# Attention on quarters of TensorE, with the sums' power on GpSimd, and a PSUM pool in the convolution part

## The chip, the cores and the metric

The kernel runs on one core of a Trainium2 chip. A core has engines that work side by side, each with its own queue of instructions that it takes in order: TensorE (called PE in the profile, its weight loads PEld) for matrix products, VectorE (DVE), ScalarE (ACT) and GpSimd (POOL) for work on elements, and SyncE (SP), which here only issues transfers. Data lies in SBUF; TensorE writes its products to PSUM, an accumulation memory of 128 partitions by 4,096 fp32 numbers, in 8 banks of 512. Engines wait for one another by semaphores.

The metric is the time of one execution on the device in microseconds (us). The median of the runs and one profiled execution are given; the profiled execution also has a span, from its first to its last recorded instruction.

## The reference

x has the shape (4, 1024, 256), four sequences of 1,024 tokens of 256 numbers; ctx has (4, 64, 256). Three blocks follow one another, each added to its input and normalised over the 256 numbers (a layer norm):

```python
# 1: Hyena, two long convolutions with gates
r = depthwise_conv3(u @ w_in.T + b_in)        # 768 channels: x0, x1, v
for n in range(2):
    y = irfft(rfft(v, 2048) * rfft(h[n], 2048))[:1024]
    v = y * x_n
out = v @ w_out.T + b_out
# 2: cross attention, 16 heads of 16 numbers, 64 keys
q, k, v = x @ Wq.T + bq, ctx @ Wk.T + bk, ctx @ Wv.T + bv
attn = softmax(einsum('bhqd,bhkd->bhqk', q, k) / 4)
out = einsum('bhqk,bhkd->bhqd', attn, v) @ Wo.T + bo
# 3: gated feed-forward, inner width 1024, with activations
#    rounded to 8 bits and weights to -1, 0, 1 times a scale
out = bitlinear(silu(bitlinear(x, wg)) * bitlinear(x, wu), wd)
```

The filter h of the first block comes from a small network of sines. In the softmax, each sum of 64 exponentials is what the weighted sum of values is divided by.

## The kernel before, in words

**The first part, lines 425 to 850.** The convolution is computed for 8 units (a sequence and half of its channels) by matrix products with tables of sines and cosines. Its stages are: `stage_j` projects and passes the result through memory for the depthwise convolution, `stage_tv` and `stage_tx` transpose, `stage_f` goes to frequencies, `stage_p` multiplies there by the filter on DVE, `stage_i0` and `stage_i1` come back, and `stage_o` applies w_out and the layer norm. The stages of neighbouring units are interleaved by a loop over units. Its instructions are issued straight through the wrapper `Queue.call` (line 61), so their rows in the profile bear L61. An fp32 matrix product takes two passes on TensorE, and the profile has a record for each.

**The second part.** When the loop reaches unit 6 (`u == NU - 2`), `nc.hold()` is called: from here on each instruction is recorded as a `Step` and not issued. The rest of the convolution (the list `rest`) is recorded together with the attention and the feed-forward of 32 tiles of 128 tokens, named by (g, t): g is a group of 512 tokens, t one of its 4 tiles. The functions per tile are:

- `att_q(g)`, line 991, once per group: transposes x1 of four tiles (`turned2`), then computes the queries. `keys(b)`, line 963, builds masked keys of each sequence on DVE, so that heads which share rows of TensorE do not mix.
- `att_s(g, t)`, line 1016: the scores by 4 matmuls, each on 64 of TensorE's 128 rows and 256 moving columns, into 2 banks; the maximum over the 64 keys and the subtraction on DVE; the exponential on ACT. The rows of the profile for these matmuls are `ps_t<-w_in,x0t` and `ps_t<-hf,x0t`, 64x256, the keys being in either buffer.
- `att_v(g, t)`, line 1040: 8 transposes of the exponentials e into PSUM, ACT's copy of them to eT (`vt<-ps_t`), and 8 matmuls with eT as the stationary side and `vblk` as the moving side, 34 columns wide: 2 heads of 16 values and a column of ones each, which gives the sum of weights (`ps_t<-hf,vt` 128x34). DVE takes the reciprocal of the 16 sums of each token (128x16) and multiplies.
- `att_o(g, t)`, line 1077: 2 transposes of the result c (`ps_t<-ident,xt`), ACT's copy to cT (`xc<-ps_t`), the product with Wo, the residual and the layer norm (`norm`, line 1067). The norm's inverse square root is a power of -0.5 on POOL, one number per token: the rows with `mhalf`.
- `ffn_x`, `ffn_h`, `ffn_d`, `ffn_o`: the rounding of the activations, the gate and up products with the silu, the down product, and the last layer norm.

All held instructions are issued by `Engines.go` and bear L82. Their order is not that of the code: `plan` (line 232) is a list scheduler. It takes a cost per instruction from `Step.cost` (line 98), keeps a clock per engine and per PSUM bank (`Clock`), allows an engine to choose among steps that could start within `SLACK`, and prefers low rank; `OFFSET` (line 278) shifts the rank of a stage, and `TABLE_RANK` counts a change of ACT's function table. The order found is written into the engines' queues; on the chip each engine keeps to it and waits at each semaphore.

**PSUM.** One tile `ps_t` holds all 8 banks (line 412). In the first part it is a ring of four pieces of 1,024 columns. In the second, scores have banks 0 and 1; the transposes and the queries banks 2 and 3; the feed-forward's products and the rest of the convolution banks 4 and 5; the small results, named by their first letter (`small`, line 859), bank 6 for a, k, p and bank 7 for the others.

Of the kernel before, what the change touches and what calls it, by code (L numbers as in the profile page):

```python
# [35 lines left out]
NPV = 49  # L36
# [156 lines left out]
class Clock:  # L193


    def __init__(self, steps, before):
        self.steps, self.before = steps, before
        self.free = dict.fromkeys(("PE", "DVE", "ACT", "POOL", "SP"), 0.0)
        self.table = None
        self.bank = [dict.fromkeys(self.free, 0.0) for _ in range(8)]  # L200
        self.end, self.start = [0.0] * len(steps), [0.0] * len(steps)
# [29 lines left out]

def plan(steps, before, rank):
# [11 lines left out]
    for _ in range(n):  # L244
        best = None
        for e, w in wait.items():
            if not w:
# [5 lines left out]
                key=lambda i: (rank[i] + (TABLE_RANK if steps[i].func not in (None, c.table) else 0.0), i),  # L253
# [14 lines left out]
def follow(steps, before, order):  # L268
# [15 lines left out]
def decoder_kernel(  # L284
# [47 lines left out]
    chalf = const.tile([P, 2], FP, name="chalf")  # L332
# [521 lines left out]
    def big(name):  # L854

        o = dict(s=0, t=1024, q=1024, e=1024).get(name[0], 2048)
        return ps_t[:, o : o + 1024]

    def small(name, dtype=FP):
        v = ps_t[:, 3072:3584] if name[0] in "akp" else ps_t[:, 3584:4096]  # L860
        return v if dtype == FP else v.bitcast(dtype)


# [27 lines left out]
    vblk = hfree[0][:, 512 : 512 + B * 8 * 34].rearrange("p (b a e d) -> p b a e d", b=B, a=8, e=2)  # L891

    nc.at = -1
    for dt in range(2):
        ps = small(f"k{dt}")
        for kt in range(2):
            mm(ps[:, 0:256], wk_sb[:, kt, dt * P : dt * P + P], cx[:, kt, :], start=kt == 0, stop=kt == 1)
        act(kT[:, dt, :], ps[:, 0:256], AF.Identity, bias=pv[:, C_BK + dt : C_BK + dt + 1])
    nc.gpsimd.memset(vblk, 0.0)
    for e in range(2):  # L900
        h = slice(64 * e, 64 * e + 64)
        nc.gpsimd.memset(vblk[h, :, :, e, DH : DH + 1], 1.0)
    for b in range(B):
        ps = small(f"v{b}")
        mm(ps[:, 0:256], ones16, brow[:, 2, :], start=True, stop=False)
        for kt in range(2):
            mm(
                ps[:, 0:256],
# [5 lines left out]
        p4 = ps[:, 0:256].rearrange("p (a e d) -> p a e d", e=2, d=DH)  # L914
        for e in range(2):
            h = slice(64 * e, 64 * e + 64)
            nc.scalar.copy(vblk[h, b, :, e, 0:DH], p4[h, :, e, :])
# [9 lines left out]
    r_mx, r_rc, r_am, r_sg, r_hm = stats(NH, 2), stats(NH, 2), stats(3, 4), stats(2, 8), stats(4, 6)  # L927
# [13 lines left out]
    r_c, r_cT = Ring(*parts(xt_t, D)), Ring(*parts(xc_t[1], D))  # L941
# [21 lines left out]
    def keys(b):  # L963

        kb[b] = r_kb().rearrange("p (k h s) -> p k h s", k=2, h=4)
        mk = pv[:, C_MK : C_MK + 4].unsqueeze(2).to_broadcast([P, 4, SKV])
        for dt in range(2):
            tt_(
                kb[b][:, dt],
                kT[:, dt, b * SKV : b * SKV + SKV].unsqueeze(1).to_broadcast([P, 4, SKV]),  # L970
# [4 lines left out]
    def turned2(src, dst, name):  # L975

        ps = big(f"t{name}")
        for kt in range(2):
            for t in range(4):
                nc.tensor.transpose(  # L980
                    ps[:, kt * 512 + t * P : kt * 512 + t * P + P], src[:, t, kt * P : kt * P + P], ident
                )
        nc.scalar.copy(dst.rearrange("p k t -> p (k t)"), ps)
# [7 lines left out]
    def att_q(g):  # L991
# [6 lines left out]
        ps = big(f"q{g}")  # L998
# [17 lines left out]
    def att_s(g, t):  # L1016

        s = gs[g]
        ps = big(f"s{g}_{t}")
# [11 lines left out]
        p3 = ps.rearrange("p (h s) -> p h s", s=SKV)  # L1031
        mx = r_mx()
        nc.vector.tensor_reduce(mx, p3, AX.X, ALU.max)
        e = r_e()[:, 0:1024].rearrange("p (h s) -> p h s", s=SKV)
        tt_(e, p3, mx.unsqueeze(2).to_broadcast([P, NH, SKV]), ALU.subtract)
        ef = e.rearrange("p h s -> p (h s)")
# [3 lines left out]
    def att_v(g, t):  # L1040
        s = gs[g]
        ps = big(f"et{g}_{t}")
        for a in range(8):
            nc.tensor.transpose(ps[:, a * P : a * P + P], s["e", t][:, a * P : a * P + P], ident)
        eT = r_eT().rearrange("p (a q) -> p a q", a=8)
        nc.scalar.copy(eT.rearrange("p a q -> p (a q)"), ps)
        av = small(f"av{g}_{t}")
        for a in range(8):
            mm(
                av[:, a * 34 : a * 34 + 34],  # L1050
                eT[:, a, :],
                vblk[:, g // 2, a].rearrange("p e d -> p (e d)"),
                start=True,
                stop=True,
            )
        a3_ = av[:, 0 : NH * 17].rearrange("p (h d) -> p h d", d=17)
        rc = r_rc()
        nc.vector.reciprocal(rc, a3_[:, :, DH])
        s["c", t] = r_c()
        tt_(  # L1060
            s["c", t].rearrange("p (h d) -> p h d", d=DH),
            a3_[:, :, 0:DH],
            rc.unsqueeze(2).to_broadcast([P, NH, DH]),
            ALU.mult,
        )
# [28 lines left out]
    def ffn_x(g, t):  # L1094
# [16 lines left out]
        ps = small(f"xqT{g}_{t}", F16)  # L1111
# [5 lines left out]
    def ffn_h(g, t):  # L1117
# [3 lines left out]
        for w, k in ((wg_q, 0), (wu_q, 1)):  # L1121
            ps = big(f"p{g}_{t}_{k}")
# [25 lines left out]
    def ffn_d(g, t):  # L1148
        s = gs[g]
        hT = s["hT", t]  # L1150
        po = small(f"po{g}_{t}")
        for c in range(8):
            mm(po[:, 0:D], hT[:, c, :], wd_q[:, c, :], start=c == 0, stop=False)

        mm(po[:, 0:D], neg16, wd_s, start=False, stop=True)
        stt(s["x2", t], po[:, 0:D], s["hs", t], s["x2", t], ALU.mult, ALU.add)
# [23 lines left out]
    space_of["rest"] = ps_t[:, 2048:3072]  # L1180
# [42 lines left out]
def _constants():  # L1223
# [16 lines left out]
    mk = (p[:, None] % 64 // DH == np.arange(4)[None, :]).astype(np.float32)  # L1240
# [67 lines left out]
```

## Time and profile before

| what | value |
| --- | --- |
| median of 3 runs | 764.66 us (764.33 to 764.86) |
| profiled execution, its own time | 765.34 us |
| its span | 763.5 us |
| mean granted TensorE clock | 0.974 |
| busy PE | 710.0 us, 93% |
| busy DVE | 651.4 us, 85% |
| busy ACT | 373.4 us, 49% |
| busy POOL | 150.3 us, 20% |

How to read it. Busy times are shares of the span; TensorE's are modelled, since matrix products are pipelined, so a busy PE need not be at its peak. A row of the groups has the line, the engine and operation, the tiles written and read, the shapes (partitions x elements per partition, type) and the count; behind the first bar the busy time and the mean duration of one in nanoseconds; behind the second the idle time of that engine just before these instructions, and which engine's work ended it. A row of the timeline has the start and the duration in us, and in brackets the idle time before it. Tiles that are used again keep the name of their first use: `small_t` holds the small numbers per token, `xt` the attention's result c, `xc` its transpose, `vt` the transposed exponentials, `tap` the exponentials, `x0t` the queries, `hf` and `w_in` the keys, `hf` also `vblk`, `x1sp` the residual stream.

### The profile page before, as it was taken

To read this page: it belongs to the slowest core of one execution; us is meant where nothing else is said; L and a number is where in the kernel's file an instruction comes from. 1 tells how busy PE (TensorE), PEld (TensorE's weight loads), DVE (VectorE), ACT (ScalarE), POOL (GpSimd) and SP (SyncE) were. 2 spreads that over 40 slices of the span, in tenths; PEclk is the share of its full clock that TensorE was granted. 3 is DMA by queue.
4 is the path that set the end of the run, shared out by engine and by line. 5 is a ranking of instruction groups with operands and counts; after the bars stand their busy time and mean duration, and the time that the engine had idled before them with its cause. 6 is when DMAs were issued, how large, how long until landed. Compare 5 with 4: busy or idle time off the path is not lost. (4 is left out here: it accounts for less than half of the span.)

```text
span 763.5 us, 9645 instructions
## 1 busy us (share of the span) xinstructions
PE 710.0 (93%) x3606; PEld 511.0 (67%) x3606; DVE 651.4 (85%) x1189; ACT 373.4 (49%) x430; POOL 150.3 (20%) x214
## 2 busy tenths in 40 slices
PE   5899599999999999998999999999999999999863
PEld 1346286868687787876788787757676767767631
DVE  3446719999999999599979997989999999999984
ACT  2712516245361525224332213687778777868631
POOL 1210211111121112112000220122222322322322
PEclk9989989999999999999999999999999999999985
DMA  8572553537470644609601000012131322121232
GB/s 282 124 133 110 121 100 65 101 56 142 69 159 16 138 83 82 112 6 177 180 10 55 1 1 1 1 36 49 43 56 36 63 43 63 29 48 41 49 70 48
DMA packets 65140, 57.29 MB, mean 75 GB/s; under 512 B 38500, under 2 KB 49252, under 8 KB 65094
## 3 DMA queue, kind: packets, MB, share of 16 engines
q0 software_dynamic: 13056, 25.17, 19.3%
q1 hardware_dynamic: 47612, 27.84, 14.2%
q10 hardware_dynamic: 4426, 3.68, 1.7%
q8 instruction: 28, 0.46, 0.2%
q14 instruction: 18, 0.15, 0.1%
HBM read 17.34 MB, written 4.19 MB: 28 GB/s over the span
## 5 line engine op out<-in xcount | busy, mean ns | idle before, releaser
L82 PE MATMUL ps_t<-hf 128*128 128x512 bf16 (+1 forms) x512 | 100.3, 334 | 16.6 <-DMA hf<-vf 7.3
L82 PEld LDWEIGHTS <-hf 128*128 128x128 bf16 (+1 forms) x512 | 48.2, 100 | 57.7 <-issue 23.2
L61 PE MATMUL ps_t<-vt,fw 128*128 128x256 f32 x384 | 85.2, 380 | 0.9 <-ACT vt L61 0.6
L61 PEld LDWEIGHTS ps_t<-vt,fw 128*128 128x128 f32 x384 | 72.8, 190 | 13.5 <-issue 2.4
L61 PE MATMUL ps_t<-xt,w_in 128*128 128x512 f32 x168 | 76.4, 607 | 5.1 <-DMA w_in<-in_w_inT 5.1
L61 POOL DMA_DIRECT2D xc<-tap x28 | 33.9, 1245 | 207.1 <-ACT tap L61 133.5
L82 POOL TENSOR_TENSOR small_t<-small_t,mhalf 128x1 f32<-128x1 f32 x64 | 36.4, 574 | 157.6 <-DVE small_t L82 155.7
L82 PEld LDWEIGHTS ps_t<-hf,vt 128*128 128x128 f32 x512 | 61.0, 192 | 8.8 <-DVE small_t L82 3.1
L82 PE MATMUL ps_t<-hf,vt 128*128 128x34 f32 x512 | 61.9, 275 | 1.9 <-DVE xt L82 0.7
L61 PEld LDWEIGHTS ps_t<-xt,w_in 128*128 128x128 f32 x168 | 32.5, 195 | 43.1 <-issue 41.9
L61 ACT ACTIVATE tap<-ps_t,tbias,pv 128x1024 f32<-128x1024 f32 x42 | 48.6, 1210 | 11.4 <-DMA xc<-tap 11.4
L61 DVE TENSOR_TENSOR q<-q 128x1024 f32<-128x1024 f32 x44 | 53.0, 1218 | 0.4
L61 DVE TENSOR_TENSOR q<-vf,hf 128x1024 f32<-128x1024 f32 (+1 forms) x33 | 51.8, 1575 | 0.6
L61 ACT ACTIVATE xc<-ps_t,cbias,pv 128x512 f32<-128x512 f32 x28 | 21.5, 778 | 61.7 <-PE ps_t L61 61.7
L82 DVE SCALAR_TENSOR_TENSOR q<-ps_t,small_t,q 128x1024 f32<-128x1024 f32 x32 | 40.9, 1278 | 7.6 <-PE ps_t L82 4.6
L82 ACT ACTIVATE vf<-q,chalf,small_t 128x1024 f32<-128x1024 f32 x32 | 39.5, 1236 | 15.8 <-POOL small_t L82 8.1
L82 ACT ACTIVATE tap<-tap 128x1024 f32<-128x1024 f32 x32 | 33.8, 1056 | 25.6 <-DVE tap L82 25.4
L61 ACT COPY vo<-ps_t 128x512 f32<-128x512 f32 x24 | 14.0, 585 | 64.1 <-PE ps_t L61 47.4
L61 PE MATMUL ps_t<-q,gi__123 128*128 128x256 f32 x192 | 45.4, 393 | 0.0
L82 ACT ACT_TABLE_LOAD x34 | 43.6, 1283 | 2.2 <-PE ps_t L82 1.6
L82 ACT ACTIVATE q<-ps_t,small_t 128x1024 f32<-128x1024 f32 x32 | 35.6, 1113 | 17.5 <-PE ps_t L82 14.4
L61 DVE TENSOR_TENSOR vf<-ps_t,vo 128x512 f32<-128x512 f32 x48 | 31.1, 683 | 14.7 <-ACT vo L61 14.7
(149 smaller groups left out, 1493.4 us busy)
## 6 DMA issues: line engine op xcount, KB each, us to landing
xc<-tap POOLq DMA_DIRECT2D x32, 512.0 KB, 5.1
x1c<-tap POOLq DMA_DIRECT2D x16, 512.0 KB, 7.1
xt<-in_xT SPq DMA_DIRECT2D x8, 512.0 KB, 6.3
x1sp<-in_x SPq DMA_DIRECT2D x8, 512.0 KB, 4.6
out_y<-v SPq DMA_DIRECT2D x32, 128.0 KB, 1.7
hf<-x1sp SPq DMA_DIRECT2D x3, 512.0 KB, 2.9
fw<-in_dftf SPq DMA_DIRECT2D x1, 1024.0 KB, 14.0
gi__123<-in_dfti SPq DMA_DIRECT2D x1, 1024.0 KB, 10.7
```

The source lines that it names most:

```text
L61: return f(*a, **k)
L82: pin(steps[i].f(*steps[i].a, **steps[i].k))
```

## The change

**PSUM of the first part.** It now comes from a pool `psa` of 4 buffers of 1,024 columns, each asked for at its use. The pool is closed when the loop reaches unit 6, and a second pool with the one tile `ps_t` of 4,096 columns is opened. The held rest of the convolution first takes pieces of it from a ring of four, later from `p_w` alone.

**PSUM of the second part.** Scores `p_s` take the first 256 columns of each of banks 0 to 3 and the transposes `p_t` the last 256. `p_w` is banks 4 and 5. Bank 6 holds `p_num` and `p_den` (`p_xq` lies over `p_den`), bank 7 `p_o` and `p_po`.

**Scores.** 8 matmuls per tile, each on 32 of TensorE's rows with 128 moving columns, the four row quarters into four banks; the masked keys are half as wide. The heads are permuted to suit (`hp` and `mk`).

**Values and sums.** eT is now the moving side, 128 columns, and the stationary side is 32 columns wide: 8 matmuls with `vone` give each head's sum of weights 16 times over, 8 with `vblk` the weighted values, each on one quarter of TensorE's columns. The result lies transposed already. ACT copies the sums, 128x256, to `rd`; POOL raises them to the power -1; DVE multiplies `p_num` by them into cT. The reciprocal on DVE, the 2 transposes of c and ACT's copy of cT are gone.

**Planner.** A change between whole, row-quarter and column-quarter matmuls costs 0.1 or 0.2; a quarter matmul counts a fourth; steps of the same kind are preferred; a wide POOL operation counts 0.52 + 0.002 n, and the constants are others.

```diff
+        self.mode = ""
+        if engine == "PE":
+            self.mode = "rows" if self.ins[0].partition_size() == 32 else "cols" * (self.out.partition_size() == 32)
...
-            if lhs.partition_size() == 64:
-                one *= 0.62
-            return (2 * max(one, 0.112) if rhs.dtype == FP else one), 0.2
+            one = 2 * max(one, 0.112) if rhs.dtype == FP else one
+
+            return (one / 4 if self.mode else one), 0.2
...
-        if self.what == "tensor_copy" or n > 64:
+        if self.what == "tensor_copy":
             return 0.1 + n * 0.00096, 0.06
-        return 0.52, 0.06
+        return 0.52 + n * 0.002 * (n > 64), 0.06
...
+        if e == "PE" and s.mode != self.mode:
+            t += 0.2 if s.mode else 0.1
+            self.mode = s.mode
...
-SLACK = {"PE": 0.00, "DVE": 0.07, "ACT": 0.76, "POOL": 0.0, "SP": 0.0}
-TABLE_RANK = 3.39
+SLACK = {"PE": 0.01, "DVE": 0.07, "ACT": 0.81, "POOL": 0.0, "SP": 0.0}
+TABLE_RANK = 2.89
 OFFSET = dict(
-    att_q=-0.40, att_s=-0.97, att_v=-0.50, att_o=0.40, ffn_x=0.28, ffn_h=-1.75, ffn_d=1.08, ffn_o=2.59, rest=-0.10
+    att_q=-1.38, att_s=-1.85, att_v=-1.26, att_o=0.37, ffn_x=0.56, ffn_h=-3.69, ffn_d=1.97, ffn_o=8.98, rest=-1.46
...
+    nc.gpsimd.memset(chalf[:, 2:3], -1.0)
+    minus = chalf[:, 2:3]
...
-    ps_t = ctx.enter_context(tc.tile_pool(name="ps", bufs=1, space=PSUM)).tile([P, 4096], FP, name="ps_t")
-    r_ps = Ring(*(ps_t[:, 1024 * i : 1024 * i + 1024] for i in range(4)))
+    psa = tc.tile_pool(name="psa", bufs=4, space=PSUM)
+    psa_p = psa.__enter__()
+
     space_of = {}
 
     def big1(name):
-        return space_of["rest"] if space_of else r_ps()
+        return space_of["rest"]() if space_of else psa_p.tile([P, 1024], FP, tag="big", name=name)
...
+                psa.__exit__(None, None, None)
+                psb = ctx.enter_context(tc.tile_pool(name="psb", bufs=1, space=PSUM))
+                ps_t = psb.tile([P, 4096], FP, name="ps_t")
+                space_of["rest"] = Ring(*(ps_t[:, 1024 * i : 1024 * i + 1024] for i in range(4)))
...
+    def quarters(o):
+
+        return ps_t[:, 0:2048].rearrange("p (b c) -> p b c", b=4)[:, :, o : o + 256]
+
+    def part(o, n, dtype=FP):
+        v = ps_t[:, o : o + n]
         return v if dtype == FP else v.bitcast(dtype)
 
+    p_s, p_t, p_w = quarters(0), quarters(256), part(2048, 1024)
+    p_num, p_den, p_xq = part(3072, 256), part(3328, 256), part(3328, 128, F16)
+    p_o, p_po = part(3584, 256), part(3840, 256)
...
+    vone = hfree[0][:, 1536:1568].rearrange("p (e d) -> p e d", e=2)
...
+        kb[b] = r_kb()[:, 0:256].rearrange("p (k h s) -> p k h s", k=2, h=2)
+        mk = pv[:, C_MK : C_MK + 2].unsqueeze(2).to_broadcast([P, 2, SKV])
...
-            for r in range(2):
-                h = slice(64 * r, 64 * r + 64)
+            for r in range(4):
+                h = slice(32 * r, 32 * r + 32)
                 mm(
-                    ps[:, r * 512 + dt * 256 : r * 512 + dt * 256 + 256],
+                    p_s[:, r, dt * P : dt * P + P],
...
-        nc.scalar.copy(eT.rearrange("p a q -> p (a q)"), ps)
-        av = small(f"av{g}_{t}")
-        for a in range(8):
-            mm(
-                av[:, a * 34 : a * 34 + 34],
-                eT[:, a, :],
-                vblk[:, g // 2, a].rearrange("p e d -> p (e d)"),
...
-        nc.vector.reciprocal(rc, a3_[:, :, DH])
...
+        nc.scalar.copy(eT.rearrange("p (r d) q -> p r (d q)", d=2), p_t)
+        for ps, w in ((p_den, None), (p_num, vblk[:, g // 2])):
+            for a in range(8):
+                h = slice(32 * (a % 4), 32 * (a % 4) + 32)
+                mm(
+                    ps[h, a // 4 * P : a // 4 * P + P],
+                    (vone if w is None else w[:, a]).rearrange("p e d -> p (e d)"),
+                    eT[:, a, :],
+                    start=True,
+                    stop=True,
+                )
+        rd = r_rd()
+        nc.scalar.copy(rd, p_den)
+        nc.gpsimd.tensor_tensor(rd, rd, minus.to_broadcast([P, D]), ALU.pow)
+        s["c", t] = r_cT()
+        tt_(s["c", t], p_num, rd, ALU.mult)
...
-        ps = small(f"o{g}_{t}")
-        for kt in range(2):
-            nc.tensor.transpose(ps[:, kt * P : kt * P + P], s["c", t][:, kt * P : kt * P + P], ident)
-        cT = r_cT()
-        nc.scalar.copy(cT, ps[:, 0:D])
-        o = ps[:, D : 2 * D]
+        cT, o = s["c", t], p_o
...
-    space_of["rest"] = ps_t[:, 2048:3072]
+    space_of["rest"] = Ring(p_w)
...
-    hp = np.arange(D).reshape(2, 2, 4, DH).transpose(1, 0, 2, 3).reshape(D)
+    hp = np.arange(D).reshape(2, 4, 2, DH).transpose(1, 0, 2, 3).reshape(D)
```

More of the change, by code (lines that the diff above doesn't have):

```diff
@@ L35 @@
 C_BIN, C_CW, C_CB, C_BQ, C_BK, C_B1, C_NT, C_SG, C_MK = 0, 6, 24, 30, 32, 34, 35, 43, 45
-NPV = 49
+NPV = 47
 class Ring:
@@ L198, in __init__ @@
         self.free = dict.fromkeys(("PE", "DVE", "ACT", "POOL", "SP"), 0.0)
-        self.table = None
+        self.table, self.mode = None, ""
         self.bank = [dict.fromkeys(self.free, 0.0) for _ in range(8)]
@@ L252, in plan @@
                 (i for i in w if t[i] <= t1),
-                key=lambda i: (rank[i] + (TABLE_RANK if steps[i].func not in (None, c.table) else 0.0), i),
+                key=lambda i: (
+                    rank[i]
+                    + (TABLE_RANK if steps[i].func not in (None, c.table) else 0.0)
+                    - (9.0 if steps[i].mode and steps[i].mode == c.mode else 0.0),
+                    i,
+                ),
             )
@@ L331, in decoder_kernel @@
     nc.gpsimd.memset(mhalf, -0.5)
-    chalf = const.tile([P, 2], FP, name="chalf")
+    chalf = const.tile([P, 3], FP, name="chalf")
     nc.gpsimd.memset(chalf[:, 0:1], MAGIC16)
     nc.gpsimd.memset(chalf[:, 1:2], -HALF)
+    nc.gpsimd.memset(chalf[:, 2:3], -1.0)
+    minus = chalf[:, 2:3]
     cmagic = const.tile([P, 2], FP, name="cmagic")
@@ L852, in decoder_kernel @@
     ]
[L854 to L860, printed above, removed]
+    def quarters(o):
+        return ps_t[:, 0:2048].rearrange("p (b c) -> p b c", b=4)[:, :, o : o + 256]
+    def part(o, n, dtype=FP):
+        v = ps_t[:, o : o + n]
         return v if dtype == FP else v.bitcast(dtype)
+    p_s, p_t, p_w = quarters(0), quarters(256), part(2048, 1024)
+    p_num, p_den, p_xq = part(3072, 256), part(3328, 256), part(3328, 128, F16)
+    p_o, p_po = part(3584, 256), part(3840, 256)
     def load_late(dst, src):
@@ L889, in decoder_kernel @@
     kT = two(hfree[0][:, 0:512])
-    vblk = hfree[0][:, 512 : 512 + B * 8 * 34].rearrange("p (b a e d) -> p b a e d", b=B, a=8, e=2)
+    vblk = hfree[0][:, 512:1536].rearrange("p (b a e d) -> p b a e d", b=B, a=8, e=2)
+    vone = hfree[0][:, 1536:1568].rearrange("p (e d) -> p e d", e=2)
     nc.at = -1
     for dt in range(2):
-        ps = small(f"k{dt}")
+        ps = p_po
         for kt in range(2):
-            mm(ps[:, 0:256], wk_sb[:, kt, dt * P : dt * P + P], cx[:, kt, :], start=kt == 0, stop=kt == 1)
-        act(kT[:, dt, :], ps[:, 0:256], AF.Identity, bias=pv[:, C_BK + dt : C_BK + dt + 1])
+            mm(ps, wk_sb[:, kt, dt * P : dt * P + P], cx[:, kt, :], start=kt == 0, stop=kt == 1)
+        act(kT[:, dt, :], ps, AF.Identity, bias=pv[:, C_BK + dt : C_BK + dt + 1])
     nc.gpsimd.memset(vblk, 0.0)
+    nc.gpsimd.memset(vone, 0.0)
     for e in range(2):
-        h = slice(64 * e, 64 * e + 64)
-        nc.gpsimd.memset(vblk[h, :, :, e, DH : DH + 1], 1.0)
+        nc.gpsimd.memset(vone[64 * e : 64 * e + 64, e, :], 1.0)
     for b in range(B):
-        ps = small(f"v{b}")
-        mm(ps[:, 0:256], ones16, brow[:, 2, :], start=True, stop=False)
+        ps = p_o
+        mm(ps, ones16, brow[:, 2, :], start=True, stop=False)
         for kt in range(2):
             mm(
-                ps[:, 0:256],
+                ps,
                 cx2[:, kt, b].rearrange("p e s -> p (e s)"),
@@ L913, in decoder_kernel @@
             )
-        p4 = ps[:, 0:256].rearrange("p (a e d) -> p a e d", e=2, d=DH)
+        p4 = ps.rearrange("p (a e d) -> p a e d", e=2, d=DH)
         for e in range(2):
             h = slice(64 * e, 64 * e + 64)
-            nc.scalar.copy(vblk[h, b, :, e, 0:DH], p4[h, :, e, :])
+            nc.scalar.copy(vblk[h, b, :, e, :], p4[h, :, e, :])
     small_t = const.tile([P, 216], FP, name="small_t")
@@ L925, in stats @@
         return Ring(*(small_t[:, at[0] - n * i - n : at[0] - n * i] for i in range(k)))
-    r_mx, r_rc, r_am, r_sg, r_hm = stats(NH, 2), stats(NH, 2), stats(3, 4), stats(2, 8), stats(4, 6)
+    r_mx, r_am, r_sg, r_hm = stats(NH, 2), stats(3, 4), stats(2, 8), stats(4, 6)
     r_n = {"b": stats(10, 4), "c": stats(10, 4)}
@@ L940, in decoder_kernel @@
     r_q, r_eT, r_e = Ring(*x0t_t), Ring(*vt_t), Ring(*tap_t)
-    r_c, r_cT = Ring(*parts(xt_t, D)), Ring(*parts(xc_t[1], D))
+    r_rd, r_cT = Ring(*parts(xt_t, D)), Ring(*parts(xc_t[1], D))
     r_x2 = Ring(*parts(x1c_t[2], D), *parts(x1c_t[0], D), *parts(x1c_t[1], D))
@@ L963, in keys @@
     def keys(b):
-        kb[b] = r_kb().rearrange("p (k h s) -> p k h s", k=2, h=4)
-        mk = pv[:, C_MK : C_MK + 4].unsqueeze(2).to_broadcast([P, 4, SKV])
+        kb[b] = r_kb()[:, 0:256].rearrange("p (k h s) -> p k h s", k=2, h=2)
+        mk = pv[:, C_MK : C_MK + 2].unsqueeze(2).to_broadcast([P, 2, SKV])
         for dt in range(2):
@@ L969, in keys @@
                 kb[b][:, dt],
-                kT[:, dt, b * SKV : b * SKV + SKV].unsqueeze(1).to_broadcast([P, 4, SKV]),
+                kT[:, dt, b * SKV : b * SKV + SKV].unsqueeze(1).to_broadcast([P, 2, SKV]),
                 mk,
@@ L975, in turned2 @@
     def turned2(src, dst, name):
-        ps = big(f"t{name}")
         for kt in range(2):
             for t in range(4):
+                i = 4 * kt + t
                 nc.tensor.transpose(
-                    ps[:, kt * 512 + t * P : kt * 512 + t * P + P], src[:, t, kt * P : kt * P + P], ident
+                    p_t[:, i // 2, i % 2 * P : i % 2 * P + P], src[:, t, kt * P : kt * P + P], ident
                 )
-        nc.scalar.copy(dst.rearrange("p k t -> p (k t)"), ps)
+        nc.scalar.copy(dst.rearrange("p k (h c) -> p (k h) c", h=2), p_t)
     def low(v):
@@ L997, in att_q @@
         s["q"] = two(r_q())
-        ps = big(f"q{g}")
+        ps = p_w
         for dt in range(2):
@@ L1018, in att_s @@
         s = gs[g]
-        ps = big(f"s{g}_{t}")
         for dt in range(2):
-            for r in range(2):
-                h = slice(64 * r, 64 * r + 64)
+            for r in range(4):
+                h = slice(32 * r, 32 * r + 32)
                 mm(
-                    ps[:, r * 512 + dt * 256 : r * 512 + dt * 256 + 256],
+                    p_s[:, r, dt * P : dt * P + P],
                     s["q"][h, dt, t * P : t * P + P],
@@ L1030, in att_s @@
                 )
[L1031 to L1036, printed above, removed]
+        p4 = p_s.rearrange("p r (h s) -> p r h s", s=SKV)
+        mx = r_mx().rearrange("p (r h) -> p r h", r=4)
+        nc.vector.tensor_reduce(mx, p4, AX.X, ALU.max)
+        e = r_e()[:, 0:1024]
+        tt_(
+            e.rearrange("p (r h s) -> p r h s", r=4, s=SKV),
+            p4,
+            mx.unsqueeze(3).to_broadcast([P, 4, 4, SKV]),
+            ALU.subtract,
+        )
+        ef = e
         act(ef, ef, AF.Exp, scale=0.25)
@@ L1041, in att_v @@
         s = gs[g]
-        ps = big(f"et{g}_{t}")
         for a in range(8):
-            nc.tensor.transpose(ps[:, a * P : a * P + P], s["e", t][:, a * P : a * P + P], ident)
+            nc.tensor.transpose(
+                p_t[:, a // 2, a % 2 * P : a % 2 * P + P], s["e", t][:, a * P : a * P + P], ident
+            )
         eT = r_eT().rearrange("p (a q) -> p a q", a=8)
-        nc.scalar.copy(eT.rearrange("p a q -> p (a q)"), ps)
-        av = small(f"av{g}_{t}")
-        for a in range(8):
-            mm(
-                av[:, a * 34 : a * 34 + 34],
-                eT[:, a, :],
-                vblk[:, g // 2, a].rearrange("p e d -> p (e d)"),
[L1053 to L1057, printed above, removed]
-        nc.vector.reciprocal(rc, a3_[:, :, DH])
[L1059 to L1065, printed above, removed]
+        nc.scalar.copy(eT.rearrange("p (r d) q -> p r (d q)", d=2), p_t)
[8 more added lines that the diff above has]
+                    stop=True,
+                )
+        rd = r_rd()
[3 more added lines that the diff above has]
+        tt_(s["c", t], p_num, rd, ALU.mult)
     def norm(r, dst, name):
@@ L1110, in ffn_x @@
         ts_(xr, x2, am[:, 2:3], MAGIC16, ALU.mult, ALU.add)
-        ps = small(f"xqT{g}_{t}", F16)
+        ps = p_xq
         for kt in range(2):
@@ L1121, in ffn_h @@
         for w, k in ((wg_q, 0), (wu_q, 1)):
-            ps = big(f"p{g}_{t}_{k}")
+            ps = p_w
             for h in range(2):
@@ L1150, in ffn_d @@
         hT = s["hT", t]
-        po = small(f"po{g}_{t}")
+        po = p_po
         for c in range(8):
-            mm(po[:, 0:D], hT[:, c, :], wd_q[:, c, :], start=c == 0, stop=False)
-        mm(po[:, 0:D], neg16, wd_s, start=False, stop=True)
-        stt(s["x2", t], po[:, 0:D], s["hs", t], s["x2", t], ALU.mult, ALU.add)
+            mm(po, hT[:, c, :], wd_q[:, c, :], start=c == 0, stop=False)
+        mm(po, neg16, wd_s, start=False, stop=True)
+        stt(s["x2", t], po, s["hs", t], s["x2", t], ALU.mult, ALU.add)
     def ffn_o(g, t):
@@ L1239, in _constants @@
     sg = np.where(p % 2 == 0, 1.0, -1.0).astype(np.float32)
-    mk = (p[:, None] % 64 // DH == np.arange(4)[None, :]).astype(np.float32)
+    mk = (p[:, None] % 32 // DH == np.arange(2)[None, :]).astype(np.float32)
     return dftf, dfti, peT, nt, np.stack([sg, -sg], axis=1), mk
```

## The prediction

> **What bounds the kernel now.** I read the page's busy line first. TensorE (PE) is busy for 93% of the span, VectorE (DVE) for 85%, and GpSimd (POOL) for only 20%.
>
> ```profile
> PE 710.0 (93%) x3606; PEld 511.0 (67%) x3606; DVE 651.4 (85%) x1189; ACT 373.4 (49%) x430; POOL 150.3 (20%) x214
> ```
>
> Then the windows by stage. Columns: stretch in us and its length, busy time and count of PE, PEld, DVE, ACT, POOL, granted TensorE clock, DMA share, GB/s. The rows are the convolution, the stretch where its rest runs beside the first attention tiles, the steady attention and feed-forward, and the end.
>
> ```profile
> 107.00:340.00 233.00, 232.73 (x1007) 180.21 (x1006) 214.61 (x251) 95.09 (x104) 40.62 (x35) 1.00 0.45 84
> 340.00:480.00 140.00, 136.35 (x714) 106.77 (x713) 126.87 (x203) 41.79 (x57) 19.76 (x21) 0.99 0.25 59
> 480.00:740.00 260.00, 247.79 (x1635) 176.34 (x1634) 247.98 (x649) 193.23 (x217) 66.65 (x117) 1.00 0.22 44
> 740.00:764.00 24.00, 8.68 (x35) 4.33 (x35) 11.19 (x24) 3.59 (x4) 5.45 (x9) 0.58 0.26 59
> ```
>
> In the convolution PE is the bound. In the steady stretch PE (247.8 of 260) and DVE (248.0) share it, and POOL works 66.7 us: it has slack, but of this size only. By the view of the tile ps_t the first matmul on values is at 397.7 us; by the timeline the last tile's begin at 725.1. So a tile takes (725.1 − 397.7)/31 = 10.56 us on average, and 38.4 us follow the last.
>
> The groups by shape carry the rest. Columns: busy us, mean ns of one, then the engine's idle time before them and what ended it.
>
> ```profile
> L82 PE MATMUL ps_t<-hf,vt 128*128 128x34 f32 x512 | 61.9, 275 | 1.9 <-DVE xt L82 0.7 <-DVE small_t L82 0.6 <-DVE x1c L82 0.5
> L82 DVE RECIPROCAL small_t<-ps_t 128x16 f32<-128x16 f32 x32 | 7.8, 244 | 2.4 <-PE ps_t L82 2.2
> L82 POOL TENSOR_TENSOR small_t<-small_t,mhalf 128x1 f32<-128x1 f32 x64 | 36.4, 574 | 157.6 <-DVE small_t L82 155.7 <-ACT vf L82 1.7
> L82 POOL TENSOR_TENSOR small_t<-small_t,mw 128x1 f32<-128x1 f32 x32 | 6.1, 191 | 80.9 <-DVE small_t L82 74.2 <-ACT q L82 3.6 <-ACT hf L82 3.0
> L82 POOL TENSOR_TENSOR ln_t<-ln_t,mhalf 128x4 f32<-128x4 f32 x4 | 4.5, 1132 | 26.5 <-DVE ln_t L82 26.5
> L61 POOL TENSOR_TENSOR ln_t<-ln_t,mhalf 128x4 f32<-128x4 f32 x4 | 4.1, 1026 | 28.7 <-DVE ln_t L61 28.7
> L82 POOL TENSOR_TENSOR q<-q 128x256 f16<-128x256 f16 x1 | 0.7, 673 | 0.1
> ```
>
> The reader is to see three prices on POOL. A power (the rows with mhalf) of 1 column takes 574 ns and of 4 columns 1,026 to 1,132. A multiplication of 1 column (with mw) takes 191. An addition of 256 columns takes 673. The timeline gives the powers undisturbed: 0.55 for 1 column, 1.01 for 4.
>
> ```profile
> 423.04 1.48 POOL L82 TENSOR_TENSOR small_t<-small_t,mhalf 128x1 f32<-128x1 f32 x1 [59.47 <-DVE small_t L82]
> 437.16 1.01 POOL L82 TENSOR_TENSOR ln_t<-ln_t,mhalf 128x4 f32<-128x4 f32 x1 [3.42 <-DVE ln_t L82]
> 462.31 0.55 POOL L82 TENSOR_TENSOR small_t<-small_t,mhalf 128x1 f32<-128x1 f32 x1 [8.47 <-DVE small_t L82]
> ```
>
> **The change part by part**
>
> *Reciprocal to POOL.* The change takes the 244 ns reciprocal of 16 columns from DVE and issues a power of −1 over 128x256 on POOL, 32 times. The trace has no power this wide. From 1 to 4 columns a power grows by (1.01 − 0.55)/3 = 0.154 us per column, so a straight line gives 0.55 + 255 × 0.154 = 39.8 us. By the two means it would be (1.132 − 0.574)/3 = 0.186 and 48.0 us: the upper bound. The lower: an addition of 256 columns (0.67) and a power's surplus over a one-column multiplication (0.55 − 0.19 = 0.36), 1.03 us. I take 39.8, because the four-column powers are the same operation and already cost nearly twice the one-column ones, while the addition is another operation and grows by only (0.673 − 0.191)/255 = 1.9 ns per column.
>
> POOL works in order and has one queue: 32 powers cannot overlap. Behind each stand the layer norms' powers, the mw multiplications and the fp16 copies; DVE waits for the result in the product p_num × rd, and behind that product stand the next max and subtraction. So POOL sets the tile. Between one power's end and the next one's start the built order puts the DVE product (0.42), a max and a subtraction (1.21 each), ACT's copy of eT (1.01) and of the sums (0.37), together 4.2, with hand-offs and POOL's own small work some 6 us. Bounds: 2.7 with the product, the two copies and eight passes of 0.107 alone; about 10 when exp with its table load and the transposes fall in too. A tile is 39.8 + 6 = 45.8 us in place of 10.56.
>
> A rule that leans against my line: the Trainium skill, *GPSIMD Engine Reference*, "3.1 Elementwise — side-by-side cycle accounting", counts about 2.6 cycles per element for an operation with two inputs. At the clock it names that is an estimate of 0.55 us plus a fixed part for 256 columns, and the sum would be the first rival's; it has no row for a power, and the two rows of powers here grow some seventy times faster than that.
>
> *Quarters of columns.* An fp32 matmul is two passes. Per tile 8 matmuls on 34 moving columns (16 passes 0.1115 us apart from start to start, 1.78 us) become 16 on a quarter of the columns with 128 moving columns. A 256-column pass takes 0.216 from start to start, so 128 take some 0.107: 32 × 0.107 = 3.4 us one after another, 0.86 if four quarters run together. The two transposes of c (2 × 0.28) and ACT's copy of cT (0.366) go.
>
> *Quarters of rows.* Per tile 4 matmuls of 64x256 (1.16 us, of which 0.83 are 4 pairs of passes, 0.208 each, side by side on the two halves) become 8 of 32x128: 16 passes of 0.107, 1.7 us one after another, 0.43 in fours. No trace here shows quarters at all: with the 0.33 us that entering and leaving the halves costs now (1.16 − 0.83), both parts and the c transposes lie between some −2 and +2 us of PE per tile. Under a POOL of 45.8 us per tile either end is hidden, as PE has 35 us of slack there; I count 0.
>
> *Keys.* Eight DVE products of 512 columns become half as wide, −1.6 us at most, hidden likewise.
>
> *PSUM pool in the first part.* The order is the same from unit 1 on. At the start i0(0)'s 12 matmuls now stand ahead of unit 1's transposes, which wait for a DMA at 96.19 with PE idle for 8.40 us. They take 12 × 0.379 = 4.55 of that wait, and the hand-offs 0.4 back: −4.2. Bounds: 0 (q is late too) and −4.6. Where the pools change, the first held matmul, at 322.95, must wait for the last reader of any bank, the DVE addition at 324.84 that ends at 326.06: between 0 and +3.1. PE idles for 2.7 us at 355 on another wait, which can take most of it up; I take +1.
>
> *Planner.* New offsets reorder the early tiles: −6 to +2 us before the first power; 0 taken.
>
> The sum. The first value matmul was at 397.7; less 3.2 from the first part, plus some 3 for the sums and their copy, the first power starts at about 397. Then 31 × 45.8 = 1,419.8, the last power 39.8, and what followed the last values, 38.4 less the 1.8 of those matmuls: 36.6. Together 397 + 1,419.8 + 39.8 + 36.6 = 1,893 span. The profiled execution took 765.34 at a span of 763.5, so 1.84 lies outside: 1,895, and the median of the runs is 0.7 under that execution: **1,894**. Its own range has 39.8 to 48.0 per power and gaps of 2.7 to 10: 1,790 to 2,280 at the corners; as the shorter rows are the undisturbed ones I use 1,780 to 2,060.
>
> **The rivals**
>
> *A, a cheap wide power: faster.* One mechanism: columns after the first few are nearly free, as in the addition. Price up to some 4 us per power: break-even is where power plus gap of 6.5 equals 10.56, that is 4 us, or 13 ns per column. For it: the addition's 1.9 ns per column. Against it: the four-column powers' 154. Then the old bound counts: 765.3 − 4.2 + 1 − 9.4 (reciprocals 7.8 and keys 1.6, on a DVE that is co-bound) − 9.2 (half of the 18.5 us that DVE waits for PE in the held part, as scores and values come sooner) = 743, between 730 and 762.
>
> *B, a cheap power, but the quarters run one after another.* PE gains 3.4 + 1.7 + 0.4 for changes of form and loses 1.78 + 1.16 + 0.56: +2.0 us per tile, with PE already 95% busy in the steady stretch, so 32 × 2.0 = 64 at most, less some 14 where PE now waits: 815. For it: no row shows two matmuls at once beyond the pairs of halves; against it: those pairs, at 0.208 for two of 0.216.
>
> *C, a power in between,* 4 to 30 us, if its loop over columns overlaps part of its work: at 12 us a tile is 18, and the end 397 + 31 × 18 + 12 + 36.6 = 1,004; 780 to 1,700 in all.
>
> *D, the reorder alone:* everything cheap and hidden, 765 less 4.2 plus up to 3: within 0.2% (about what these runs can tell from no change) only by accident.
>
> **How the numbers follow.** The straight line gets 0.72; A 0.17; C 0.07; B and the accident of D 0.04 together. Predicted is the likeliest, 1,894. From 740 to 2,060 the range holds most of A, and C, B and the main case but for its upper corner; the likeliest case's own range is 1,780 to 2,060. Faster 0.17 (A), same 0.01, slower 0.82.
>
> **What would show it.** Right: a group of 32 powers on 128x256 with a mean near 39,800 ns, POOL busy nearly throughout from 400 us on, DVE's product released by POOL xt, PE and DVE mostly idle, about 46 us from tile to tile. The 8.40 us wait at 96.19 would be halved, and PE would wait up to 3 us for DVE x1sp at its first held matmul. Wrong: a power near 1 us, PE still over 85% busy in the steady stretch; then the quarters' matmuls, with the distance from start to start, tell A from B. My forecast falls with one number, the slope of the power over columns, which I draw from two points 3 columns apart and stretch to 256.
>
> A second rule, on what stands beside: the Trainium skill, *SBUF — State Buffer*, "Who interferes with whom", has a DVE operation with two SBUF inputs contend with a GpSimd one. The power at 423.04 took 1.48 beside such a DVE operation, 0.55 without; by that rule the wide power would also delay the convolution's remaining DVE products, which no run here shows.

## The result, and the profile after

The changed kernel takes 2,032.96 us (median of 4 runs, 2,032.18 to 2,035.03) against 764.5 us before: a ratio of 2.660, 95% interval 2.655 to 2.664. Its profiled execution took 2,033.33 us with a span of 2,031.6.

The busy line of the page after, and windows of it (columns as before):

```profile
PE 735.3 (36%) x4310; PEld 501.9 (25%) x4310; DVE 647.1 (32%) x1157; ACT 379.4 (19%) x434; POOL 1469.6 (72%) x248
```

```profile
340.00:480.00 140.00, 73.42 (x451) 58.75 (x449) 63.10 (x73) 21.85 (x33) 79.62 (x6) 0.77 0.19 49
740.00:1900.00 1160.00, 240.79 (x1986) 151.69 (x1985) 216.96 (x531) 186.02 (x202) 1010.29 (x122) 0.60 0.04 9
```

The work of DVE and ACT has hardly changed in amount (647 and 379 us, from 651 and 373), but POOL's has risen from 150 to 1,470 us. In the long stretch POOL is busy for 1,010 of 1,160 us and the other engines for a fifth each. The granted TensorE clock stands at 0.60 there.

Groups by shape of the changed kernel:

```profile
L82 POOL TENSOR_TENSOR xt<-xt,chalf 128x256 f32<-128x256 f32 x32 | 1318.8, 41211 | 102.7 <-ACT xt L82 102.7
L82 DVE TENSOR_TENSOR xc<-ps_t,xt 128x256 f32<-128x256 f32 x32 | 13.6, 425 | 1257.8 <-POOL xt L82 1257.8
L82 PE MATMUL ps_t<-gi__123,q 128*128 128x256 f32 x128 | 32.8, 418 | 3.1 <-DVE x1sp L61 3.1
```

The first row is the power of -1: 32 times 41.2 us, 1,318.8 us. The second is the product behind it, for which DVE stood idle 1,257.8 us until POOL was done. The third has the wait at the change of pools.

One step from power to power in the timeline of the changed kernel (start, duration, work, idle time before):

```profile
1163.23 41.15 POOL L82 TENSOR_TENSOR xt<-xt,chalf 128x256 f32<-128x256 f32 x1 [1.06 <-ACT xt L82]
...
1204.42 0.42 DVE L82 TENSOR_TENSOR xc<-ps_t,xt 128x256 f32<-128x256 f32 x1 [38.36 <-POOL xt L82]
...
1206.69 1.86 PE L82 MATMUL ps_t<-hf 128*128 128x256 f16 x8 [39.43 <-DVE x1c L82]
...
1208.78 1.91 PE L82 MATMUL ps_t<-w_in,xc 128*128 128x256 f32 x4
...
1210.48 1.25 PE L82 MATMUL ps_t<-hf 128*128 128x512 bf16 x4
...
1211.66 1.08 PE L82 MATMUL ps_t<-vt,hf 128*32 128x128 f32 x32
...
1212.81 0.37 ACT L82 COPY xt<-ps_t 128x256 f32<-128x256 f32 x1 [6.55 <-PE ps_t L82]
...
1213.55 41.15 POOL L82 TENSOR_TENSOR xt<-xt,chalf 128x256 f32<-128x256 f32 x1
```

The power ends at 1,204.38; the next begins 9.2 us later. In between TensorE, whose queue is in order, has the down product of another tile, the product with Wo, half of a gate product, and only then the quarters for the next sums. In this step TensorE first waited until 1,206.69, 2.3 us past the power's end, for DVE's x1c. The quarters themselves are quick: 32 passes in 1.08 us, where 16 took 1.87 before. The timeline of the kernel before has these 16 passes, and a down product of the same eight passes:

```profile
561.61 1.87 PE L82 MATMUL ps_t<-hf,vt 128*128 128x34 f32 x16
...
564.59 1.05 PE L82 MATMUL ps_t<-hf 128*128 128x256 f16 x8
```

### The profile page after: what moved, and what is told of

Read it like the earlier page. It is cut to its first block, busy times and chain, and to the rows that moved or that the text cites. A ratio compares the mean times of both kernels' runs of the same rounds, so it can differ in the third digit from the quotient of the medians.

```text
span 2031.6 us, 11089 instructions
## 1 busy us (share of the span) xinstructions
PE 735.3 (36%) x4310; PEld 501.9 (25%) x4310; DVE 647.1 (32%) x1157; ACT 379.4 (19%) x434; POOL 1469.6 (72%) x248
## 5 line engine op out<-in xcount | busy, mean ns | idle before, releaser
L82 POOL TENSOR_TENSOR xt<-xt,chalf 128x256 f32<-128x256 f32 x32 | 1318.8, 41211 | 102.7 <-ACT xt L82 102.7
L82 DVE TENSOR_TENSOR xc<-ps_t,xt 128x256 f32<-128x256 f32 x32 | 13.6, 425 | 1257.8 <-POOL xt L82 1257.8
L82 PE MATMUL ps_t<-hf 128*128 128x256 f16 (+1 forms) x512 | 130.1, 400 | 259.7 <-DVE x1c L82 79.9
L82 PEld LDWEIGHTS <-hf 128*128 128x128 f16 (+1 forms) x512 | 57.3, 117 | 309.4 <-issue 239.5
L82 ACT ACTIVATE vf<-q,chalf,small_t 128x1024 f32<-128x1024 f32 x32 | 39.6, 1236 | 438.2 <-DVE small_t L82 357.2
L82 PE MATMUL ps_t<-w_in,xc 128*128 128x256 f32 x128 | 50.6, 526 | 190.5 <-DVE xc L82 151.6
L82 PE MATMUL ps_t<-vt,hf 128*32 128x128 f32 x1024 | 43.2, 320 | 156.4 <-ACT hf L82 78.9
L61 PE MATMUL f<-vt,fw 128*128 128x256 f32 x384 | 84.9, 379 | 1.1 <-ACT vt L61 1.1
L61 PE MATMUL pj<-xt,w_in 128*128 128x512 f32 x168 | 76.6, 608 | 4.2 <-DMA w_in<-in_w_inT 4.2
L61 PEld LDWEIGHTS f<-vt,fw 128*128 128x128 f32 x384 | 72.9, 190 | 13.3 <-issue 2.4
L82 PE MATMUL ps_t<-ident,tap 128*128 128x128 f32 x256 | 43.4, 316 | 78.4 <-ACT vt L82 42.4
L82 PEld LDWEIGHTS ps_t<-ident,tap 128*128 128x128 f32 x256 | 35.3, 165 | 88.0 <-ACT vt L82 44.1
```

What stands on the lines that cost most here:

```text
L61: return f(*a, **k)
L82: pin(steps[i].f(*steps[i].a, **steps[i].k))
```

## The experiments

All ratios are to runs of the kernel before on the same chip in the same session, whose medians were 764.3 us (for the powers of 64 and 16 columns, the pool alone and the first reciprocal), 766.25 us (for the power of 4 columns, the repriced power, the power in the old form and the rows alone) and 766.7 us (for the repriced reciprocal and the columns alone). Runs of different sessions are best compared by these ratios.

**1. The power's width.** Three kernels take the power over the first 64, 16 or 4 of the 256 columns and leave the other sums as they are, so that the attention there is not divided. The planner is told 1.03 us for it in each, so every engine's order is that of the changed kernel.

```diff
-        nc.gpsimd.tensor_tensor(rd, rd, minus.to_broadcast([P, D]), ALU.pow)
+        nc.gpsimd.tensor_tensor(rd[:, 0:64], rd[:, 0:64], minus.to_broadcast([P, 64]), ALU.pow)
...
+        if n == 64:
+            return 1.032, 0.06
```

> The changed kernel, its order of work unchanged, with the power taken over the first 64 of 256 columns only (the other 192 sums are left as they are, so the attention is divided by nothing there). Theory 1 (a power costs the same for every column, 0.159 us by 41.14 at 256): one power 0.55 + 63 x 0.159 = 10.6 us; a tile 10.6 and a gap of 6 to 9 us, so 386 + 31 x 18.1 + 10.6 + 39 = 997 us (930 to 1,050). Rival (a wide operand costs a block of its own, whatever the columns, or its cost grows faster than the columns): a power near 2 to 5 us, or the gap and not the power sets the tile, 760 to 850 us.

> As the run with 64 columns, with 16. The power: 0.55 + 15 x 0.159 = 2.9 us. Theory 1 with the break-even of 4 us per power: POOL no longer sets the tile, and the time lies under that of the kernel before, 735 to 764 us. Rival (the round through ACT, POOL and back to DVE costs more than the power itself, so that the gap of 9 us between powers stays): 386 + 31 x 12 + 3 + 39 = 800 us.

> The changed kernel, order unchanged, with the power over 4 of the 256 columns (the other sums are left as they are). It takes 1.01 us then, what the planner has assumed for the whole. Theory 1 (only the length of the power costs): 783 us was measured with 2.9 us; 32 tiles save 1.9 us each at most, so down to 722, and with half of it off the path 752. Theory 2 (something else in the quarters' form holds the attention back, as TensorE was busy for 208 and DVE for 218 of 260 us in the steady stretch with 2.9 us, so neither was the bound): 765 to 783 us, with TensorE and DVE idle again.

The view of the tile xt on POOL gives the power in each (durations min/median/max in ns, first and last start in us). The changed kernel:

```profile
L82 POOL TENSOR_TENSOR xt<-xt,chalf x32: 41122/41142/42143, 385.9 to 1951.4; 128x256 f32<-128x256 f32 x32
```

64 columns:

```profile
L82 POOL TENSOR_TENSOR xt<-xt,chalf x32: 10529/10538/11537, 386.7 to 1000.6; 128x64 f32<-128x64 f32 x32
```

16 columns:

```profile
L82 POOL TENSOR_TENSOR xt<-xt,chalf x32: 2897/2912/3912, 386.9 to 737.0; 128x16 f32<-128x16 f32 x32
```

4 columns:

```profile
L82 POOL TENSOR_TENSOR xt<-xt,chalf x32: 1006/1018/2020, 389.3 to 701.7; 128x4 f32<-128x4 f32 x32
```

The cost is a straight line: (41.14 − 2.91)/240 = 0.159 us per column from 16 to 256, (10.54 − 2.91)/48 = 0.159 from 16 to 64, (2.91 − 1.02)/12 = 0.158 from 4 to 16. No block and no overlap shows up to 256 columns.

| columns | power, us | time, us | ratio to before |
| --- | --- | --- | --- |
| 256 | 41.14 | 2,032.96 | 2.660 (2.655 to 2.664) |
| 64 | 10.54 | 1,052.43 (one run) | 1.377 |
| 16 | 2.91 | 782.78 | 1.023 (1.020 to 1.026) |
| 4 | 1.02 | 741.58 | 0.967 (0.963 to 0.971) |

So the power is the whole loss. With 1 us for it the changed kernel is 3.3% below the one before, but with all columns of sums but 4 left undivided, and 1.3% of it is the first part's pool by itself (experiment 2). With 64 columns a step from power to power is (1,000.6 − 386.7)/31 = 19.8 us, 9.2 more than the power; with 256 it is (1,951.4 − 385.9)/31 = 50.5, 9.3 more; with 16 it is 11.3, 8.3 more. With 4 columns, where POOL no longer sets the pace, the same reckoning still leaves (701.7 − 389.3)/31 − 1.07 = 9.0 us. So the gap is about what a tile takes in this order without the long power; in the step shown above, DVE was busy for 7.2 and TensorE for 6.6 of its 9.1 us. With 64 columns the gap lies just above the 6 to 9 us expected and the time 2 us above theory 1's range; with 4 the time is inside it. With 16 both expectations were missed (735 to 764, and 800); experiment 4 shows the planner's price to be most of the reason.

**2. The first part's pool alone.** The kernel before with the two edits for PSUM in the first part; attention and planner constants as before.

```diff
-    ps_t = ctx.enter_context(tc.tile_pool(name="ps", bufs=1, space=PSUM)).tile([P, 4096], FP, name="ps_t")
+    psa = tc.tile_pool(name="psa", bufs=4, space=PSUM)
+    psa_p = psa.__enter__()
...
+                psa.__exit__(None, None, None)
+                psb = ctx.enter_context(tc.tile_pool(name="psb", bufs=1, space=PSUM))
+                ps_t = psb.tile([P, 4096], FP, name="ps_t")
```

> The kernel before with only the first part's PSUM taken from a pool that is closed at unit 6, and a ring of four pieces for the rest's first steps; the attention as before. Theory P (the start gained in the first part is kept, since TensorE is the bound there and behind it): the first held matmul at some 314 us in place of 323, 3 us of it given back as a wait for the last reader, so 764.5 - 6 = 758 us (755 to 761). Rival Q (it is given back at the change of pools or by a worse order of the held part): 763 to 768 us.

754.81 us, ratio 0.987 (0.985 to 0.989): theory P, with a gain of 9.5 us, 3 more than expected (754.81 lies just under the range). The view of PE's waits up to 110 us, in the kernel before (waited for, us in total, times, longest):

```profile
PE ps_t L61 <- DMA xc<-tap: 8.4, 1, 8.4
PE ps_t L61 <- DMA w_in<-in_w_inT: 5.1, 1, 5.1
PE ps_t L61 <- ACT tap L61: 3.8, 1, 3.8
PE ps_t L61 <- DMA x1sp<-in_peT: 3.6, 1, 3.6
```

and with the pool:

```profile
PE pj L61 <- DMA w_in<-in_w_inT: 5.9, 1, 5.9
PE z L61 <- DMA x1sp<-in_peT: 3.5, 1, 3.5
PE i L61 <- DVE q L61: 2.7, 1, 2.7
```

Two waits are gone: the 8.4 us for the DMA, of which 2.7 come back as a wait of i0(0) for q, and another of 3.8 us for ACT in the filter's products, near 39.6 us. Over 30 to 70 us the granted clock is 1.00 where it was 0.91. The last matmul of a forward transform in the first part starts at 301.6 us against 314.1, 12.5 earlier; the wait at the change of pools then takes 3.1 back. This version leaves nothing out and is below both kernels; no other complete version here is below the kernel before by more than the noise.

**3. The reciprocal on DVE.** ACT's copy and the power give way to one instruction that reads PSUM. In a second version the planner is told 1.70 us for it in place of 0.33.

```diff
-        nc.scalar.copy(rd, p_den)
-        nc.gpsimd.tensor_tensor(rd, rd, minus.to_broadcast([P, D]), ALU.pow)
+        nc.vector.reciprocal(rd, p_den)
```

> The changed kernel with the wide power on POOL and ACT's copy of the sums replaced by one reciprocal on DVE, 128x256, straight from PSUM. Theory 1 (the power is the whole loss, the quarters run side by side): the time falls below the kernel before, 743 us (725 to 765) if the reciprocal takes about 0.42 us like a product of the same shape; some 785 if it takes 1.75 us, the line through the 1-column (0.15) and 16-column (0.244) reciprocals, as that is 1.3 us more on DVE per tile. Theory 2 (the quarters or the new order cost time too, hidden behind the power): above 790 us even with a reciprocal near 0.42.

> The version with the reciprocal of 128x256 on DVE, with the planner told 1.70 us for it in place of 0.33 (1.75 was measured). Theory 1 (the order had no room for it, as with the power of 16 columns, where the true price brought 25 us): 765 to 778 us. Rival (DVE's added work itself is the cost: 55.9 us of reciprocals in place of 7.8, on an engine that is busy for 86% already with the cheap power): 785 to 792 us, as before.

The group in the version with the wrong price:

```profile
L82 DVE RECIPROCAL xt<-ps_t 128x256 f32<-128x256 f32 x32 | 55.9, 1748 | 3.3 <-PE ps_t L82 2.7 <-ACT vf L82 0.6
```

790.25 us, ratio 1.033 (1.030 to 1.036), and 775.06, 1.013 (1.009 to 1.016), with the true price. The reciprocal takes 1.75 us, so the first lies at the dear branch of theory 1 (785). The price in the planner is worth 15 us. What remains is work: the windows of the priced version have DVE at 254.65 of 260 us from 480 to 740 us.

```profile
480.00:740.00 260.00, 207.13 (x2024) 132.88 (x2025) 254.65 (x576) 175.92 (x179) 60.51 (x104) 0.97 0.19 40
```

TensorE now has 53 us to spare there, but the quarters hand out 256 columns of sums where the old form had 16, and DVE pays for them.

**4. The planner's price for the power.** The run with 16 columns again (the other sums as they are), planned with 2.95 us.

> The run with 16 columns again, but the planner is told 2.95 us for that power in place of 1.03, so that the order makes room for it. Theory 1 (the order was planned for a power that is three times as fast, and waits arise from that): 755 to 770 us. Rival (the order does not matter, the chain through the power does): 778 to 790 us, as with the old order.

758.00 us, ratio 0.989 (0.985 to 0.992), against 782.78 in the unchanged order. The same power of 2.9 us costs 25 us less (3.5% by the ratios) when the order makes room for it: theory 1.

**5. The power in the old form.** In the kernel with the pool alone, the 16 sums per token go to POOL; the planner is told 2.95 us.

```diff
-        nc.vector.reciprocal(rc, a3_[:, :, DH])
+        nc.scalar.copy(rc, a3_[:, :, DH])
+        nc.gpsimd.tensor_tensor(rc, rc, minus.to_broadcast([P, NH]), ALU.pow)
```

> The kernel with the pool alone, and there the reciprocal of 16 columns moved from DVE to POOL: ACT copies the 16 sums, POOL raises them to the power -1. By the line 0.55 + 15 x 0.159 = 2.95 us per tile on POOL, which has some 190 of 260 us free. Theory 1 (a power of 3 us fits beside a tile of 8 us): DVE loses 7.8 us of work, 747 to 757 us. Rival (the round DVE - ACT - POOL - DVE of 4 us delays the tile, as no other work is ready): 765 to 790 us.

788.52 us, ratio 1.029 (1.025 to 1.032), 34 us above the pool alone: the time is the rival's. From 480 to 740 us POOL is busy for only 124 of 260:

```profile
480.00:740.00 260.00, 229.63 (x1449) 162.03 (x1467) 219.11 (x540) 180.09 (x220) 124.08 (x126) 0.97 0.20 41
```

POOL has half its time free and DVE lost work, and still both PE and DVE are busy less than before. That the round itself delays the tile by so much is not shown: between 310 and 740 us DVE's product waited for the power only five times, 7.8 us in all.

```profile
DVE xt L82 <- POOL small_t L82: 7.8, 5, 3.6
```

The planner's order changed with the edit too, and its constants were chosen for the old form; how much of the 34 us is the order's was not separated.

**6. The quarters one at a time.** First the rows alone: pool, scores and PSUM banks 0 to 5 as in the changed kernel, `att_v` and `att_o` from the kernel before, with constants chosen anew.

```diff
-    p_num, p_den, p_xq = part(3072, 256), part(3328, 256), part(3328, 128, F16)
-    p_o, p_po = part(3584, 256), part(3840, 256)
+    p_av, p_po = part(3072, 272), part(3072, 256)
+    p_oo, p_xq, p_o = part(3584, 512), part(3584, 128, F16), part(3584, 256)
```

> The pool in the first part and the scores on quarters of the rows, in the four shared banks; values, sums, the reciprocal of 16 columns and the transposes of c as in the kernel before; planner constants chosen anew for this form. TensorE saves 1.14 - 0.73 = 0.4 us per tile, 13 us in all, DVE 1.6 us for the narrower keys. Theory 1 (those savings are on the path of co-bound engines): 740 to 752 us, below the 754.8 of the pool alone. Theory 2 (scores and transposes now lie in the same four banks, so that the next scores wait until ACT has read the transposes): 755 to 785 us.

764.05 us (760.82 to 770.97), ratio 0.997 (0.994 to 1.001): no gain over before, and 9 us lost against the pool alone, although TensorE is busy for 695.6 us in place of 706.4. The time fits theory 2, but its wait hardly shows: from 310 to 740 us TensorE waited for ACT's copy of the transposes 2.7 us in all.

```profile
PE ps_t L82 <- ACT vt L82: 2.7, 2, 1.5
```

I also tried theory 2's condition from the other side: the columns alone, with scores and transposes in banks of their own and the power over 4 columns (the other sums as they are).

```diff
-    p_s, p_t, p_w = quarters(0), quarters(256), part(2048, 1024)
+    p_s, p_w = part(0, 1024), part(2048, 1024)
+    p_t = part(1024, 1024).rearrange("p (b c) -> p b c", b=4)
...
-            for r in range(4):
-                h = slice(32 * r, 32 * r + 32)
+            for r in range(2):
+                h = slice(64 * r, 64 * r + 64)
```

> The run with the power over 4 columns again, with the scores on halves of the rows into two banks of their own, as in the kernel before, and the transposes in two others; values and sums stay on quarters of the columns (the sums beyond 4 columns are again left as they are). Theory 2 of the run with the rows alone (scores and transposes in the same banks hold the tile back, more than the 0.4 us per tile saves): below the 741.6 us, 728 to 738. Theory 1 (quarters of the rows are worth their 13 us of TensorE when the values do not bind): 745 to 756 us.

753.78 us, ratio 0.986 (0.979 to 0.993): 12 us above the 741.58 with both, as theory 1 has it. So sharing the banks does not seem to cost more than the rows bring, and theory 2 gets no support. How much of the 12 us is the rows' own stays open: this run keeps the planner constants that were chosen for both quarters together, and experiments 3 and 4 show that an order can be worth 15 to 25 us. By the ratios, the pool alone stands at 0.987, with both quarters 0.967, with the columns alone 0.986, with the rows alone 0.997: the quarters bring 2% together, the columns alone nothing that these runs can tell, and the rows alone lose 1%. Both runs with the columns leave nearly all of the division out (the reciprocals took 7.8 us of DVE before), so that their ratios are not a gain of a complete kernel; the best complete version with both quarters is the one of 775.06 us. Why the rows lose when the values stay in the old form is open: the constants of the order differ in that run as well as the form, the granted clock from 480 to 700 us was 0.97 against 1.00 with the pool alone, and I have no run that holds these fixed.

## Why the prediction was right

**The mechanism and its size.** I took the straight line through the powers of 1 and 4 columns, 39.8 us; the wide power took 41.14. The slope was 0.159 us in place of 0.154. Before the result no row went beyond 4 columns; the runs with 16 and 64 show that the line holds in between. The rule of the Trainium skill that I had weighed against it (*GPSIMD Engine Reference*, "3.1 Elementwise — side-by-side cycle accounting", some 2.6 cycles per element with two inputs) does not carry over to a power: at the page's clock the measured column is an estimate of 190 cycles.

**The sum.** The median came 139 us above the 1,894 forecast, inside the likeliest case's own range. By its terms, in spans:

| term | predicted | measured | difference |
| --- | --- | --- | --- |
| start of the first power | 397 | 385.9 | −11 |
| 32 powers | 1,273.6 | 1,318.8 | +45 |
| 31 gaps between them | 186 (6 each) | 287.8 (9.3 each) | +102 |
| after the last power | 36.6 | 39.1 | +2 |

The gaps are the term that was mis-sized. "Between one power's end and the next one's start the built order puts" DVE's product, a max and a subtraction and two copies: I counted DVE and ACT, and not what stands in TensorE's queue ahead of the next sums. In the step shown above that is the wait of 2.3 us for x1c, the down product, the Wo product and half of a gate product, in a stretch whose granted clock was 0.60: the down product there took 1.86 us in place of 1.05. The upper bound of 10 held for the mean, not for each gap: 12 of the 31 are longer. The first two, 20.7 and 20.0 us, hold work of the convolution's rest; without them the mean is 8.5.

**The first part.** The wait at the change of pools came as said, 3.1 us, and I took 1 for it. The gain ahead of it was 12.5, not 4.2. The 8.40 us wait was not "halved" but gone, with 2.7 us of it back at another place: the 12 matmuls put ahead of the transposes are 24 passes, which took 7.13 us with the pool alone, and not 12 × 0.379 = 4.55. I had not seen the 3.82 us wait in the start's filter products, which the new order also removes, nor that the clock would stay up.

**Rival A** falls, as a wide power is not cheap. Its time for a power of some 1 us, 743 us, is near the 741.6 measured with 4 columns, but partly by luck: the pool alone brought 9.5 us where A's sum had 3.2, so that its other terms, 18.6 us, came to some 13 to 15. **Rival B** falls: 32 passes in 1.08 us cannot run one after another at 0.107 each. **The break-even** of 4 us per power was too high for this order: 2.9 us already gave 783. A straight line between the runs with 4 and 16 columns crosses the time before at 1.02 + 1.89 × (764.5 − 741.6)/(782.8 − 741.6) = 2.1 us, since the gap was 8.3 us there and not 6.5. With the true price in the planner a power of 2.9 us gave 758.

**What stood beside.** I had said that the power might delay the remaining products on DVE. It is the other way round, as the last section shows.

## What to carry to other kernels

A power on POOL is priced by its columns: 0.159 us for each column of 128 partitions, so it suits one number per token and not a matrix. Before a layout is turned, count how wide each later elementwise step becomes: here TensorE's gain made 16 columns of reciprocals into 256, which cost 41 us on POOL and 1.75 on DVE in place of 0.24. And an order written out by a planner is only as good as its prices; a price wrong by 2 us per tile cost 25 us, without any engine being full.

## What the runs showed of the hardware that I had not expected

**A power that starts beside a DVE operation on two SBUF tiles is held up by what remains of that operation; one that starts within the power is not held up.** From the timeline of the changed kernel, POOL and then DVE:

```profile
385.86 42.14 POOL L82 TENSOR_TENSOR xt<-xt,chalf 128x256 f32<-128x256 f32 x1 [34.58 <-ACT xt L82]
448.73 41.55 POOL L82 TENSOR_TENSOR xt<-xt,chalf 128x256 f32<-128x256 f32 x1 [2.16 <-ACT xt L82]
```

```profile
385.76 1.22 DVE L82 TENSOR_TENSOR pr<-vf,hf 128x1024 f32<-128x1024 f32 x1
...
448.06 1.22 DVE L82 TENSOR_TENSOR pr<-vf,hf 128x1024 f32<-128x1024 f32 x1
```

Against the median of 41.14, the first power is 1.00 us longer, with 1.12 of the DVE operation left at its start, and the second 0.41, with 0.55 left. The same pairs recur with 64 and 16 columns (maxima 11.54 and 3.91 against 10.54 and 2.91). In the run with 16 columns and the true price, DVE operations that start inside the power take their usual 1.2 us:

```profile
389.29 3.91 POOL L82 TENSOR_TENSOR xt<-xt,chalf 128x16 f32<-128x16 f32 x1 [34.45 <-ACT xt L82]
```

```profile
389.19 1.22 DVE L82 TENSOR_TENSOR pr<-vf,hf 128x1024 f32<-128x1024 f32 x1
390.32 1.24 DVE L82 TENSOR_TENSOR q<-vf,hf 128x1024 f32<-128x1024 f32 x1
391.48 1.21 DVE L82 TENSOR_TENSOR q<-q,pr 128x1024 f32<-128x1024 f32 x1
```

The Trainium skill (*SBUF — State Buffer*, "Who interferes with whom") says that a DVE operation with two SBUF inputs contends with a POOL operation that reads SBUF. The rows agree as far as the power has to wait; they do not show the power holding up DVE. DVE operations with only one SBUF input leave no such mark: in the changed kernel the power at 605.85 us began with 0.98 us left of a subtraction that reads PSUM and took 41.14 us, as usual.

**DVE's reciprocal is far slower per column than its product.** 244 ns for 16 columns and 1,748 for 256 make 6.3 ns per further column, while a product of 256 columns took 425 in all.
